# A graph layer on one core: W_tp for two groups in TensorE's column halves, placing in one pass, keys by DMA, 355 picked tiles

## The chip, the core and the metric

The kernel runs on one core of one Trainium2 chip. A core has TensorE (PE in the profile; its weight loads are PEld), VectorE (DVE), ScalarE (ACT), GpSimd (POOL) and SyncE (SP, which here only issues DMAs). The metric is the device time of one execution in microseconds; less is better. PE writes its sums to PSUM[...]; the kernel names a bank by a tag, and what is written next under a tag waits until the last reader of the tile before it is done.

## The reference

One layer of message passing over 6,250 nodes of 64 features and 200,000 edges sorted by their target, with a gate from each node's noise value, a residual and a norm over the features.

```python
w = jax.nn.silu(edge_attr @ W1 + b1) @ W2 + b2              # 200000 x 9
h_src = features[src]                                       # 200000 x 64
msg = jnp.einsum('ef,em,fmg->eg', h_src, edge_sh * w, W_tp)
agg = jax.ops.segment_sum(msg, dst, num_segments=N) / jnp.sqrt(jnp.float32(AVG_DEG))
emb = jax.nn.silu(c_noise[:, None] @ Wn1 + bn1) @ Wn2 + bn2
gamma, beta = jnp.split(emb, 2, axis=-1)
x = _layernorm(x + agg * (1.0 + gamma) + beta)
```

All values are 32-bit floats. `AVG_DEG` is 16.

## The kernel before

The 200,000 edges are 1,563 tiles of 128 edges, and 16 tiles make a group: 98 groups (`NBLK`), the last of 11 tiles. Loop `i` works on three groups at once: the hidden layer of group i + 2, the edge weights of group i + 1, the sums of group i and the projection of an older one. The order of instructions on each engine is the order in which the code is written (`manual_schedule`), so each engine's queue is laid out by hand.

**Rows of the source nodes.** A tile needs 128 rows of x. They come in three ways. POOL gathers a tile with one indirect DMA (`gather`, L91), six groups ahead (`AHEAD`) into seven buffers, so that a gather for group i + 6 needs the windows of group i - 1 to be done. Every sixth group (`SPG`) has one tile whose rows SP loads one by one (`load_rows`, L106), 22 rows in an iteration. And the last three tiles of a group (`Q`, `picked`) are picked on PE (`pick`): x lies in SBUF, split in two float32r numbers `xs`; a one-hot mask of the row within a block (`hot_k`, L464, on DVE) times `xs` gives seven candidates per feature, in 14 matmuls of 448 columns (L482); DVE then keeps one of seven (`xm`, L491) and adds up (L493) into the group's rows `hs`. The keys that the masks compare with are spread over the partitions by a matmul of ones with two bfloat16 parts of the key (`keys`, L458); the node gate (`gate`, L357) is done in the same bank.

**Per group.** `hidden` (L405, bank p1) and its Silu on ACT (L413); `second` (L422, bank s); `weights`: two transposes (L432), the product with sh (L438) and with a one-hot of 8 target positions (L444) on DVE. `windows` (L511): for each tile, rows times weights, 16 matmuls of 64 columns that write the two halves of the partitions in turn; ACT copies the sums to `zt` (L521). `project` (L537): five products of `zt` with `wtc2`, the two-at-a-time form of W_tp, each moving 64 columns; the result `r` is copied by ACT (L542). `place` (L559): two products with a one-hot `c` (L544) carry the 128 window sums of the group to two blocks of 128 nodes, and DVE adds them to `acc`, which holds all nodes (L563). `finish` gates, adds the residual and normalises two blocks of nodes (`finish_nodes`, L622 to L639): nine instructions on DVE and a square root on ACT, whose table differs from Silu's and is loaded each time (L635); the loop does this in every fourth iteration, after the second pick.

A 32-bit product runs as two passes, a float32r product and a transpose as one; the counts of the profile show it (490 projection products stand there as 980).

`pick(g, t, other)` takes the small products of other steps, one after each second matmul, so that they lie between pick matmuls. In iteration i the order on PE is: pick 0 of group i + 1 with the placing of i - 2, the keys of i + 2 and the gate between its matmuls; hidden i + 2; second i + 1; windows i; pick 1 with the weights of i + 1 and the projection of i - 1; pick 2. `setup` does the same for the first groups and splits x; `reach` tests once that the windows suffice (else a general path, not taken here, does all the work).

```python
for i in range(NBLK):
    if i + AHEAD < NBLK:
        gather(i + AHEAD)
    ...
    pick(i + 1, 0, [place(i - 2)] + ([keys(i + 2, i - 2)] if i + 2 < NBLK else []))
    ...
    hidden(i + 2)
    ...
    second(i + 1)
    ...
    windows(i)
    ...
    pick(i + 1, 1, [weights(i + 1), project(i - 1)])
    ...
    pick(i + 1, 2)
```

Of the kernel before, what the change touches and what calls it, by code (L numbers as in the profile page):

```python
# [9 lines left out]
BF16 = mybir.dt.bfloat16  # L10
# [18 lines left out]
Q = 3  # L29
# [15 lines left out]
def lo_block(g):  # L45

    return (g - 1) // 2


def picked(g):  # L50

    return Q

# [6 lines left out]
def gnn_resnorm_kernel(ctx: ExitStack, tc: tile.TileContext, x, src, dst, dst_row, ea, sh, cn,  # L60
# [18 lines left out]
    with ExitStack() as fast:  # L79
# [28 lines left out]
        acc = keep.tile([P, NJ, F], F32)  # L108
        ident = keep.tile([P, P], F32)
        w2p = keep.tile([P, D], F32)  # L110
# [7 lines left out]
        ones2 = keep.tile([P, P], BF16)  # L118
        kr2 = [keep.tile([P, LB, Q, P], BF16, name=f"kr{k}") for k in range(2)]
        zt = [keep.tile([P, 5, KB, W], F32, name=f"zt{k}") for k in range(2)]  # L120
# [7 lines left out]
        kd = dram.tile([2, C, P], BF16, name="kd")  # L128
# [7 lines left out]
        def setup(temp):  # L136
# [51 lines left out]
            nc.vector.tensor_scalar(ident, nf[:, 0:P], pf, None, op0=ALU.is_equal)  # L188
            zero = temp.tile([P, 1], F32)
            nc.vector.memset(zero, 0.0)  # L190
            for k in range(2):
                nc.vector.memset(kr2[k], 0.0)
            nc.vector.memset(ones2, 0.0)
            nc.vector.memset(ones2[0:2], 1.0)
            for k in range(2):
                nc.vector.memset(zt[k][F:P, 4], 0.0)
                nc.vector.memset(ht[k][H:H + 1], 1.0)
# [9 lines left out]
            acc_r = acc.rearrange("p j f -> p (j f)")  # L207
            s_f, kp, kh, rest, t0, t1 = [acc_r[:, k * C:(k + 1) * C] for k in range(6)]
# [12 lines left out]
            nc.vector.tensor_scalar(kh, ti[1], float(P), None, op0=ALU.mult)  # L221
            for c0 in range(0, C, P):
                n = min(P, C - c0)
                p_kt = psum.tile([P, 2, P], F32, tag=("s", "r", "s")[c0 // P], name=f"p_kt{c0}")
                for i, half in enumerate((kp, kh)):
                    nc.tensor.matmul(p_kt[0:n, i, :], half[:, c0:c0 + n], ident, start=True, stop=True)
                kt = temp.tile([P, 2, P], BF16, name=f"kt{c0}")
                nc.scalar.copy(kt[0:n], p_kt[0:n])
                nc.sync.dma_start(kd[:, c0:c0 + n, :].rearrange("i c e -> c i e"), kt[0:n])
# [36 lines left out]
            def between(h):  # L266
# [5 lines left out]
                elif h == 1:  # L272
                    for f in keys(0, -1):
                        f()
# [29 lines left out]
            for f in keys(1, -1):  # L304
                f()
# [13 lines left out]
            nc.scalar.copy(acc_r, zero.to_broadcast([P, NJ * F]))  # L319
            pick(0, 2)  # L320
# [35 lines left out]
        def gate(j, pe):  # L356
            nc.tensor.matmul(pe, ht[j // 4 % 2][:, j % 4], wn2a, start=True, stop=True)  # L357
# [5 lines left out]
        def finish(j0, j1):  # L363
            finish_nodes(nc, late, eps, acc[:, j0:j1, :], gam[:, j0:j1, :], xb[:, j0:j1, :],
                         out_v[:, j0:j1, :], j0)
# [25 lines left out]
        def load_keys(g):  # L391
            n = min(LB, NBLK - g)
            kr = kr2[g // LB % 2]
            nc.sync.dma_start(kr[0:2, 0:n].rearrange("i g t e -> i (g t) e"), kd[:, g * Q:(g + n) * Q, :])
# [56 lines left out]
        def keys(g, j):  # L451

            pk = psum.tile([P, Q + 1, P], F32, tag="r", name=f"pk{g}")
            q = picked(g)

            def part(k):
                if k == 0:
                    nc.tensor.matmul(pk[:, 0:q, :].rearrange("p t e -> p (t e)"), ones2,  # L458
                                     kr_t.pop(g).rearrange("i t e -> i (t e)"), start=True, stop=True)
                else:  # L460
                    gate(j, pk[:, Q, :])
# [62 lines left out]

        r, hot = {}, {}

        def project(g):

            if not 0 <= g < NBLK:
                return []  # L530
# [283 lines left out]
```

## Time and profile before

| | |
|---|---|
| time, median of 3 runs | 1590.99 us (1590.33 to 1592.33) |
| the profiled execution: its time, its span | 1590.71 us, 1588.9 us |
| mean granted TensorE clock | 0.961 |
| DMA | 85.42 MB, mean 54 GB/s |
| PE, 100 to 300 us: busy | 191.42 of 200 us |
| PE, 310 to 1540 us: busy | 1092.56 of 1230 us |
| POOL gathers | 1,253 |
| picked tiles | 294 |

The page gives busy time by engine, the chain of work that ended last and the costliest groups of instructions. In a group's line stand: line, engine, operation, output <- inputs, shape, count, then busy time and mean ns of one, then the idle time of the engine just before them and what ended it. A line of the timeline gives start and length in us, engine, line, operation and shape, and in brackets the idle time before it. PE's matmuls are pipelined: the length of a line is longer than the step from one start to the next, and the step is what PE pays. Idle time called "issue" is time in which the engine waited for nothing that the profile shows.

### The profile page before, as it was taken

Reading aid. Unit: us, or ns where it says so; the run is one execution under the profiler, and the core shown is the slowest. Engines: PE = TensorE matmul, PEld = TensorE weight load, DVE = VectorE, ACT = ScalarE, POOL = GpSimd, SP = SyncE. Lnnn points to the kernel's source line nnn. Section 1 sums busy time; section 2 is a strip of 40 time slices with the busy share of each in tenths; the row PEclk is TensorE's granted clock in tenths of the full one; section 3 lists DMA queues with packets and bytes.
Section 4 is the critical chain, followed back from the end, with each engine's and each line's share of the span. In section 5 each row is a group of like instructions: output and inputs, shape, how many; then the busy total and the mean of one; then the engine's idle time right before and its main releaser. Section 6 shows DMA issues by size and latency. Waiting matters only on the chain.

```text
span 1588.9 us, 33055 instructions
## 1 busy us (share of the span) xinstructions
PE 1407.5 (89%) x10206; PEld 1143.1 (72%) x10206; DVE 992.6 (62%) x1611; ACT 473.1 (30%) x1187; POOL 1186.0 (75%) x1262
## 2 busy tenths in 40 slices
PE   5999999988989888989898989888889899888886
PEld 3777778767777777777676767676777777776765
DVE  6676667665656565665665656656566666565664
ACT  4323223323232323232322323323223232322232
POOL 7777777777777777777777777777777777777773
PEclk9999999999999999999999999999999999999998
DMA  5312222221211121212111221121111211211110
GB/s 155 84 48 50 62 50 54 58 50 50 61 50 50 45 66 45 50 50 61 48 47 45 52 57 47 47 62 46 45 47 47 62 46 47 62 47 45 47 46 20
DMA packets 86199, 85.42 MB, mean 54 GB/s; under 512 B 37625, under 2 KB 52013, under 8 KB 86014
## 3 DMA queue, kind: packets, MB, share of 16 engines
q0 software_dynamic: 40096, 41.14, 11.7%
q1 hardware_dynamic: 45156, 40.44, 8.4%
q8 instruction: 83, 1.36, 0.4%
q10 hardware_dynamic: 762, 1.64, 0.3%
q14 instruction: 102, 0.84, 0.2%
HBM read 81.35 MB, written 1.78 MB: 52 GB/s over the span
## 4 chain that ended last, share of the span: by engine, by line
PE 33%; POOL 32%; issue 14%; DMA 10%; SPq 7%; DVE 2%; ACT 1%; POOLq 0%; ACTq 0%; DVEq 0%
POOL hs L91 32%; PE px L482 21%; DMA hs<-in_x_dram,src_i 9%; SPq L106 4%; PE pz L511 4%; PE pr L537 2%; PE p L405 2%; SPq L101 2%; PE p L422 1%; PE p L432 1%; PE pd L559 1%; DMA ea<-in_ea_dram 1%; DVE xm L491 0%; DVE hs L493 0%; PE pk L458 0%
## 5 line engine op out<-in xcount | busy, mean ns | idle before, releaser
L91 POOL DMA_INDIRECT hs<-in_x_dram,src_i x1253 | 1184.7, 945 | 382.6 <-issue 347.3
L482 PE MATMUL px<-xs,hot_k 128*128 128x448 f32 x4116 | 1100.4, 400 | 3.2 <-DVE xs L299 3.2
L482 PEld LDWEIGHTS px<-xs,hot_k 128*128 128x128 f32 x4116 | 717.9, 196 | 62.1 <-DVE xs L299 3.6
L491 DVE SCALAR_TENSOR_TENSOR xm<-li,jl,px 128x448 f32<-128x448 f32 x294 | 199.1, 677 | 213.0 <-PE px L482 211.2
L464 DVE TENSOR_TENSOR hot_k<-pk,nk 128x2688 fp32r<-128x2688 f32 x98 | 289.4, 2953 | 4.6 <-PE pk L458 4.6
L413 ACT ACTIVATE st<-p,b1c 128x1024 f32<-128x1024 f32 x98 | 109.1, 1114 | 560.1 <-PE p L405 559.9
L511 PE MATMUL pz<-a,hs 128*64 128x72 f32 x3126 | 135.0, 245 | 134.0 <-DMA hs<-in_x_dram,src_i 79.7
L521 ACT COPY zt<-pz 64x160 f32<-64x160 f32 (+2 forms) x784 | 213.4, 272 | 128.9 <-PE pz L511 110.8
L511 PEld LDWEIGHTS pz<-a,hs 128*64 128x64 f32 x3126 | 121.1, 151 | 177.5 <-issue 161.6
L438 DVE TENSOR_TENSOR p<-p,sh 128x72 f32<-128x72 f32 x196 | 47.3, 241 | 296.0 <-PE p L432 224.3
L537 PEld LDWEIGHTS pr<-wtc,zt 128*128 128x128 f32 x980 | 190.0, 196 | 20.8 <-ACT zt L521 5.2
L493 DVE TENSOR_REDUCE hs<-xm 128x64 f32<-128x448 f32 x294 | 182.3, 620 | 10.1
L537 PE MATMUL pr<-wtc,zt 128*128 128x64 f32 x980 | 165.0, 252 | 5.0 <-ACT zt L521 5.0
L444 DVE TENSOR_TENSOR a<-oh,p 128x1152 f32<-128x1152 f32 x98 | 132.6, 1354 | 3.3
L405 PE MATMUL p<-ea,w1bd 64*128 64x512 f32 x392 | 113.5, 657 | 5.6 <-DMA ea<-in_ea_dram 5.5
L542 ACT COPY r<-pr 128x64 f32<-128x64 f32 x98 | 20.8, 212 | 261.3 <-PE pr L537 261.3
L559 PEld LDWEIGHTS pd<-r,c 128*128 128x128 f32 x388 | 73.1, 190 | 7.3 <-ACT r L542 1.0
L422 PEld LDWEIGHTS p<-st,w2p 128*32 128x32 f32 x784 | 15.6, 109 | 74.3 <-issue 72.1
L559 PE MATMUL pd<-r,c 128*128 128x64 f32 x388 | 64.6, 249 | 0.7 <-ACT r L542 0.7
L422 PE MATMUL p<-st,w2p 128*32 128x256 f32 x784 | 63.5, 396 | 0.0
L432 PE MATMUL p<-ident,p2s 128*128 128x128 f32 x196 | 58.9, 301 | 3.9 <-ACT p2s L425 3.8
L413 ACT ACT_TABLE_LOAD x23 | 29.5, 1283 | 94.7 <-PE p L405 94.7
(103 smaller groups left out, 456.6 us busy)
## 6 DMA issues: line engine op xcount, KB each, us to landing
hs<-in_x_dram SPq DMA_DIRECT2D x2048, 0.2 KB
ea<-in_ea_dram SPq DMA_DIRECT2D x49, 512.0 KB
hs<-in_x_dram,src_i POOLq DMA_INDIRECT x1253
sh<-in_sh_dram SPq DMA_DIRECT2D x49, 144.0 KB
cb<-cn_d SPq DMA_DIRECT2D x12, 128.0 KB
out_dram<-o SPq DMA_DIRECT2D x24, 64.0 KB
gam<-in_x_dram ACTq DMA_DIRECT2D x2, 448.0 KB
dst_i<-in_dst_dram SPq DMA_DIRECT2D x1, 784.0 KB
```

The source lines that it names most:

```text
L91: hs_dma[g] = [nc.gpsimd.indirect_dma_start(out=hs[g][:, t - g * KB, :], out_offset=None, in_=x, in_offset=bass.IndirectOffsetOnAxis(ap=sr ...
L405: nc.tensor.matmul(p1[:, i, :], w1bd[i * 64:(i + 1) * 64, :], e[i * 64:(i + 1) * 64, :], start=True, stop=True)
L413: nc.scalar.activation(st[g], p1_t.pop(g), AF.Silu, bias=b1c)
L444: nc.vector.tensor_mul(a[g], oh_t.pop(g)[:, :, None, :].to_broadcast([P, KB, M, W]), sw.unsqueeze(3).to_broadcast([P, KB, M, W]))
L464: nc.vector.tensor_tensor(hot_k[g][:, 0:q], pk[:, 0:q].unsqueeze(2).to_broadcast([P, q, J, P]), nk[:, None, :, None].to_broadcast([P, q, J ...
L482: nc.tensor.matmul(px.rearrange("p f l -> p (f l)"), hot_k[g][:, t, h, :], xs[i][:, h].rearrange("p f l -> p (f l)"), start=(h == 0 and i ...
L491: nc.vector.scalar_tensor_tensor(xm, li[:, None, :].to_broadcast([P, F, J]), jl[:, c:c + 1], px, op0=ALU.is_equal, op1=ALU.mult)
L493: nc.vector.tensor_reduce(hs[g][:, tiles(g) - q + t, :], xm, AX.X, ALU.add)
L511: mm = nc.tensor.matmul(pz[v * F:(v + 1) * F, k // 2].rearrange("p m w -> p (m w)"), hsg[:, k0 + k, :], ag[:, k0 + k].rearrange("p m w -> ...
L521: nc.scalar.copy(z[h * F:(h + 1) * F, 0:5 - h, k0 + v:k0 + n:2, :].rearrange("p m k w -> p k m w"), pz[v * F:(v + 1) * F, 0:(n + 1 - v) // ...
L537: nc.tensor.matmul(pr[g], z[:, c].rearrange("p k w -> p (k w)"), wtc2[:, c, :], start=(c == 0), stop=(c == 4))
L559: nc.tensor.matmul(pd[g][:, j, :], hot[g][:, j * P:(j + 1) * P], r[g], start=True, stop=True)
```

## The change

- `Q` becomes 4, and `picked` gives 3 for three groups of eight and 4 for the other five: 355 picked tiles in all, 1,192 gathers.
- The keys are stored as one float16 number each, and SP's load spreads them over all partitions; ACT copies them to PSUM (`keys`), and the masks are made for one pick at a time (`hots`), two ahead of pick 0 of the iteration and the rest behind it.
- `project` works for two groups, in every second iteration, right behind the windows. W_tp is now the loaded operand (64 columns) and `zt` (four of them now) the moving one: group h writes half h of the partitions of bank p1, which the hidden layer uses too. ACT copies the 128 x 128 result, PE transposes it (`turn`), and `halves` splits it into two float32r numbers that lie side by side.
- `place` multiplies each group's two halves with its one-hot, 256 nodes at once, and both groups add up in PSUM. The upper 128 nodes are carried to the next pair, and the lower ones are complete (`yt`): `acc` goes.
- `bring` turns a block of nodes back and adds the two halves, with two stacked identities, and `finish` reads it from PSUM. Two blocks are finished in every fourth iteration, now within pick 0.
- `nodes` holds gate, placing and bringing of an iteration in one tile of bank s, the bank that `second` writes next.

```diff
-Q = 3
+Q = 4
...
+def pair(q):
+    return [g for g in (2 * q - 1, 2 * q) if 0 <= g < NBLK]
...
-    return Q
+    return Q - (3 * g % 8 < 3)
...
+            kf = s_f
+            nc.vector.tensor_add(kf, kp, kh)
...
+                nc.tensor.transpose(p_kt[0:n], kf[:, c0:c0 + n], ident)
...
+                nc.sync.dma_start(kd[c0:c0 + n, :], kt[0:n])
...
-                    for f in keys(0, -1):
-                        f()
+                    keys(0)
+                    hots(0, 0, Q)
...
+            keys(1)
+            hots(1, 0, Q)
...
+            for t in range(2, Q):
+                pick(0, t)
...
         def gate(j, pe):
-            nc.tensor.matmul(pe, ht[j // 4 % 2][:, j % 4], wn2a, start=True, stop=True)
             nc.vector.tensor_scalar(gam[:, j, :], pe[:, 0:F], 1.0, 0.25, op0=ALU.add, op1=ALU.mult)
             nc.vector.tensor_add(xb[:, j, :], xb[:, j, :], pe[:, F:2 * F])
...
-        def finish(j0, j1):
-            finish_nodes(nc, late, eps, acc[:, j0:j1, :], gam[:, j0:j1, :], xb[:, j0:j1, :],
-                         out_v[:, j0:j1, :], j0)
+        def finish(j0, j1, sums):
+            y = late.tile([P, j1 - j0, F], F32, tag="y", name=f"y{j0}")
+            finish_nodes(nc, late, eps, sums, y, gam[:, j0:j1, :], xb[:, j0:j1, :], out_v[:, j0:j1, :], j0)
...
         def load_keys(g):
             n = min(LB, NBLK - g)
-            kr = kr2[g // LB % 2]
-            nc.sync.dma_start(kr[0:2, 0:n].rearrange("i g t e -> i (g t) e"), kd[:, g * Q:(g + n) * Q, :])
+            kr = loads.tile([P, LB, Q, P], F16, tag="kr", name=f"kr{g}", bufs=2)
+            nc.sync.dma_start(kr[:, 0:n].rearrange("p g t e -> p (g t e)"),
+                              rows(kd[g * Q:(g + n) * Q, :].rearrange("c e -> (c e)"), P))
...
-        def keys(g, j):
-            pk = psum.tile([P, Q + 1, P], F32, tag="r", name=f"pk{g}")
-            q = picked(g)
...
-                if k == 0:
-                    nc.tensor.matmul(pk[:, 0:q, :].rearrange("p t e -> p (t e)"), ones2,
...
-                    gate(j, pk[:, Q, :])
...
+        pk_t = {}
+        def keys(g):
+            pk_t[g] = psum.tile([P, Q, P], F32, tag="r", name=f"pk{g}")
+            nc.scalar.copy(pk_t[g][:, 0:picked(g), :], kr_t.pop(g))
+        def hots(g, t0, t1):
+            for t in range(t0, min(t1, picked(g))):
+                hot_k[g, t] = late.tile([P, J, P], F32R, tag="hot_k", name=f"hot_k{g}_{t}", bufs=7)
+                nc.vector.tensor_tensor(hot_k[g, t], pk_t[g][:, t, None, :].to_broadcast([P, J, P]),
+                                        nk.unsqueeze(2).to_broadcast([P, J, P]), op=ALU.is_equal)
...
-                    nc.tensor.matmul(px.rearrange("p f l -> p (f l)"), hot_k[g][:, t, h, :],
+                    nc.tensor.matmul(px.rearrange("p f l -> p (f l)"), hot_k[g, t][:, h, :],
...
-            z = zs[g] = zt[g % 2]
+            z = zs[g] = zt[:, g % 4]
...
-        r, hot = {}, {}
-        def project(g):
-            if not 0 <= g < NBLK:
+        r, hot, carry, yt = {}, {}, {}, {}
+        def halves(q, pr):
+            n = len(pair(q))
+            r[q] = work.tile([P, 2, 2, F], F32R, tag="r", name=f"r{q}")
+            nc.scalar.copy(r[q][:, 0:n, 0], pr)
+            nc.vector.tensor_sub(r[q][:, 0:n, 1], pr, r[q][:, 0:n, 0].bitcast(F32))
+            for g in pair(q):
+                hot[g] = work.tile([P, 2 * P], F32R, tag="c", name=f"c{g}")
+                nc.vector.tensor_scalar(hot[g], nf, nid[:, g:g + 1], None, op0=ALU.is_equal)
+        def project(q):
+            gs = pair(q)
+            pt = psum.tile([P, 2, 4 * P], F32, tag="p1", name=f"pt{q}")
+            z = [zs.pop(g).rearrange("p c k w -> p c (k w)") for g in gs]
+            if len(gs) == 1:
+                for c in range(5):
+                    nc.tensor.matmul(pt[:, 0, 0:F], z[0][:, c], wtc2[:, c, :], start=(c == 0), stop=(c == 4))
+                halves(q, pt[:, 0, 0:F].unsqueeze(1))
                 return []
-            pr = {}
...
-                    pr[g] = psum.tile([P, F], F32, tag="r", name=f"pr{g}")
-                nc.tensor.matmul(pr[g], z[:, c].rearrange("p k w -> p (k w)"), wtc2[:, c, :],
-                                 start=(c == 0), stop=(c == 4))
...
-        def place(g):
...
+            for c in range(5):
+                for h in range(2):
+                    nc.tensor.matmul(pt[h * F:(h + 1) * F, 0, 0:P], wtc2[:, c, :], z[h][:, c],
+                                     start=(c == 0), stop=(c == 4))
+            rt = work.tile([P, P], F32, tag="rt", name=f"rt{q}")
+            nc.scalar.copy(rt, pt[:, 0, 0:P])
+            def turn():
+                nc.tensor.transpose(pt[:, 1, 0:P], rt, ident)
+                halves(q, pt[:, 1, 0:P].rearrange("p (g f) -> p g f", g=2))
+            return [lambda: None, lambda: None, turn]
+        def place(q, pd):
+            gs = pair(q)
+            def part(k):
+                nc.tensor.matmul(pd, r[q][:, k].rearrange("p s f -> p (s f)"), hot.pop(gs[k]),
+                                 start=(k == 0), stop=(k == len(gs) - 1))
+                if k == len(gs) - 1:
+                    r.pop(q)
+                    if q > 0:
+                        yt[q - 1] = work.tile([P, P], F32, tag="yt", name=f"yt{q}", bufs=3)
+                        nc.vector.tensor_add(yt[q - 1], pd[:, 0:P], carry.pop(q - 1))
+                    if q < NJ:
+                        carry[q] = work.tile([P, P], F32, tag="carry", name=f"carry{q}")
+                        nc.scalar.copy(carry[q], pd[:, P:2 * P])
+            return [lambda k=k: part(k) for k in range(len(gs))]
...
+        def bring(j0, j1, py):
             def part(j):
-                if j == js[0]:
-                    pd[g] = psum.tile([P, 2, F], F32, tag="s", name=f"pd{g}")
-                nc.tensor.matmul(pd[g][:, j, :], hot[g][:, j * P:(j + 1) * P], r[g], start=True, stop=True)
-                if j == js[-1]:
-                    hot.pop(g), r.pop(g)
-                    b0, b1_ = kb + js[0], kb + js[-1] + 1
-                    nc.vector.tensor_add(acc[:, b0:b1_, :], acc[:, b0:b1_, :], pd[g][:, js[0]:js[-1] + 1, :])
...
-        done = 0
+                nc.tensor.matmul(py[:, j - j0], yt.pop(j), ident2, start=True, stop=True)
+                if j == j1 - 1:
+                    finish(j0, j1, py[:, 0:j1 - j0])
+            return [lambda j=j: part(j) for j in range(j0, j1)]
+        def nodes(i):
+            ps = psum.tile([P, 4, P], F32, tag="s", name=f"ps{i}")
+            parts = []
+            if 0 <= i - 2 < NJ:
+                def product(j=i - 2):
+                    nc.tensor.matmul(ps[:, 2], ht[j // 4 % 2][:, j % 4], wn2a, start=True, stop=True)
+                parts.append(product)
+            if i % 2 == 0 and i >= 2:
+                parts += place(i // 2 - 1, ps[:, 0:2].rearrange("p a n -> p (a n)"))
+            j = (i - 5) // 2
+            if i % 2 == 1 and i >= 5 and j % FB == FB - 1:
+                parts += bring(j + 1 - FB, j + 1, ps[:, 3].rearrange("p (j f) -> p j f", f=F))
+            if 0 <= i - 2 < NJ:
+                parts.append(lambda: gate(i - 2, ps[:, 2]))
+            return parts
...
@@ -582,7 +614,12 @@
                 for g in SPG:
                     if 0 < g - i <= AHEAD:
                         load_rows(g, (AHEAD - g + i) * SPR)
-                pick(i + 1, 0, [place(i - 2)] + ([keys(i + 2, i - 2)] if i + 2 < NBLK else []))
+                if i + 2 < NBLK:
+                    keys(i + 2)
+                    hots(i + 2, 0, 2)
+                pick(i + 1, 0, [nodes(i)])
+                if i + 2 < NBLK:
+                    hots(i + 2, 2, Q)
                 if 3 <= i <= 5:
                     reach(i - 3)
                 if i + 2 < NBLK:
@@ -591,25 +628,32 @@
                     second(i + 1)
                 if i < NBLK - 2:
                     windows(i)
+                turn = project(i // 2) if i % 2 == 1 else []
                 if i % 4 == 1 and i - 1 < NJ:
                     gate_hidden(i - 1)
                 if i + 1 < NBLK:
-                    pick(i + 1, 1, [weights(i + 1), project(i - 1)])
-                else:
-                    for f in project(i - 1) + place(i - 1):
+                    pick(i + 1, 1, [weights(i + 1), turn])
+                for t in range(2, Q):
+                    pick(i + 1, t)
+                if i == NBLK - 1:
+                    for f in turn:
                         f()
-                ready = max(lo_block(i if i == NBLK - 1 else i - 1), 0)
-                while ready - done >= (FB if ready < NJ - 1 else 1):
-                    finish(done, min(done + FB, ready))
-                    done = min(done + FB, ready)
-                pick(i + 1, 2)
+                    ps = psum.tile([P, 4, P], F32, tag="s", name="ps_l")
+                    for f in place(i // 2, ps[:, 0:2].rearrange("p a n -> p (a n)")):
+                        f()
+                    py = psum.tile([P, FB, F], F32, tag="r", name="py_l")
+                    for f in bring(NJ - 3, NJ - 1, py):
+                        f()
                 if i >= NBLK - 2:
                     windows(i)
                 if i == NBLK - 2:
                     sums(i + 1)
-            for f in project(NBLK - 1) + place(NBLK - 1):
+            project(NBLK // 2)
+            ps = psum.tile([P, 4, P], F32, tag="s", name="ps_n")
+            for f in place(NBLK // 2, ps[:, 0:2].rearrange("p a n -> p (a n)")):
                 f()
-            finish(done, NJ)
+            for f in bring(NJ - 1, NJ, psum.tile([P, 1, F], F32, tag="r", name="py_n")):
+                f()
...
-def finish_nodes(nc, work, eps, y, gam, xb, out, tag):
+def finish_nodes(nc, work, eps, sums, y, gam, xb, out, tag):
     n = y.shape[1]
-    nc.vector.tensor_mul(y, y, gam)
+    nc.vector.tensor_mul(y, sums, gam)
     nc.vector.tensor_add(y, y, xb)
...
```

## The prediction

> **What bounds the kernel now.** I read the busy shares first, then the costliest groups, the chain that ended last, the timeline of a dense stretch and that of the end.
>
> ```profile
> PE 1407.5 (89%) x10206; PEld 1143.1 (72%) x10206; DVE 992.6 (62%) x1611; ACT 473.1 (30%) x1187; POOL 1186.0 (75%) x1262
> ...
> PE 33%; POOL 32%; issue 14%; DMA 10%; SPq 7%; DVE 2%; ACT 1%; POOLq 0%; ACTq 0%; DVEq 0%
> ...
> L91 POOL DMA_INDIRECT hs<-in_x_dram,src_i x1253 | 1184.7, 945 | 382.6 <-issue 347.3
> L482 PE MATMUL px<-xs,hot_k 128*128 128x448 f32 x4116 | 1100.4, 400 | 3.2 <-DVE xs L299 3.2
> L464 DVE TENSOR_TENSOR hot_k<-pk,nk 128x2688 fp32r<-128x2688 f32 x98 | 289.4, 2953 | 4.6 <-PE pk L458 4.6
> L511 PE MATMUL pz<-a,hs 128*64 128x72 f32 x3126 | 135.0, 245 | 134.0 <-DMA hs<-in_x_dram,src_i 79.7
> ```
>
> POOL looks 75% busy and is full: busy plus the idle before its gathers is 1184.7 + 382.6 = 1567.3 us of 1588.9, and that idle is "issue", not a wait. One gather costs 1567.3/1253 = 1.2508 us. PE looks fuller, but waits in the windows (L511) for gathered rows. So POOL sets the pace: 12.8 gathers, 16.0 us a group.
>
> How much PE has to spare is read where it is not waiting, in the first 300 us, where it works off a late start:
>
> ```profile
> 224.96 1.22 PE L511 MATMUL pz<-a,hs 128*64 128x72 f32 x32
> 227.65 0.33 PE L537 MATMUL pr<-wtc,zt 128*128 128x64 f32 x2
> 228.28 0.33 PE L537 MATMUL pr<-wtc,zt 128*128 128x64 f32 x2
> 230.32 3.54 PE L482 MATMUL px<-xs,hot_k 128*128 128x448 f32 x16
> 233.70 0.33 PE L559 MATMUL pd<-r,c 128*128 128x64 f32 x2
> 237.08 1.13 PE L405 MATMUL p<-ea,w1bd 64*128 64x512 f32 x4
> 238.14 0.64 PE L422 MATMUL p<-st,w2p 128*32 128x256 f32 x8
> 238.71 1.22 PE L511 MATMUL pz<-a,hs 128*64 128x72 f32 x32
> ```
>
> From windows to windows 13.75 us, and starts give prices: a pick's matmul (233.70 - 230.32)/16 = 0.211 us, so a pick of 14 is 2.96; a projection product, 0.63 less two pick matmuls, 0.21; the hidden layer 1.06; the second 0.57; the windows 1.15. The same reading gives 0.21 for a placing product, 0.15 for the keys, 0.27 for the node gate and 0.09 for a transpose.
>
> ```profile
> 1545.91 1.22 PE L511 MATMUL pz<-a,hs 128*64 128x72 f32 x32
> 1566.57 1.22 PE L511 MATMUL pz<-a,hs 128*64 128x72 f32 x32
> 1571.34 0.66 PE L559 MATMUL pd<-r,c 128*128 128x64 f32 x4 [0.35 <-ACT r L542]
> 1576.71 2.40 PE L537 MATMUL pr<-wtc,zt 128*128 128x64 f32 x10 [3.68 <-ACT zt L521]
> ```
>
> After the windows of group 95, at 1545.9, PE runs dense once more; from there to the end are 43.0 us.
>
> **What the Trainium skill says.** "TensorE: Matmul & The Clock Gate", Part 3, lets matmuls with different column tiles run at once, and its section on LDWEIGHTS prices a load by columns, P/1.2 ns. The trace agrees with the second: a projection pass, loading 128 columns and moving 64, takes 0.21/2 = 0.105 us, where the page gives 107 ns. For the first it agrees in part: the windows, 64-column halves in turn, take 1.15/32 = 36 ns a pass, far below 105, not half of the page's 53 ns for a load. "TensorEngine Tiling (Array Packing)", Key Properties, says that changing the tiling mode drains the array; the new block stands right behind the windows, which use the same halves. "ScalarE: Activation LUTs", "What ACT_TABLE_LOAD costs", gives 1283 ns for the load alone; the trace's mean is 1283. "TensorE", Part 1, lets the clock fall after an idle window of about 3.4 us; here it was 0.66 after a wait from 836 to 839 us and 1.00 after one of 2.6 us at 823.
>
> **The change, part by part.**
>
> *Picks.* 294 become 355, groups of 3 and 4. POOL loses 61 gathers, 61 x 1.2508 = 76.3 us. PE gains 61 x 2.96 = 180 us. DVE gains 61 x (xm 0.68 + reduce 0.62 + hot 1.0, a third of L464's 2.95) = 140 us, to some 1130 of 1500: it keeps up, but its order matters below.
>
> *Projection.* 97 x 5 products of 0.21 (102 us) become 48 blocks of ten products in column halves, two passes each, 128 columns moved. At the windows' 36 ns a block is 20 x 36 = 0.72 us; stretched by 128/72, 1.28. I take 0.9; bounds 0.7 and 1.5. A turn is one transpose, 0.09. Its copies on ACT and DVE lie beside the picks that follow: the transpose comes only after five pick steps, 2.1 us. Without that cover some 0.6 us a pair, 30 in all.
>
> *Placing and nodes.* 194 placing products of 0.21 become 98 single passes moving 256 columns. The nearest row, the pick's matmul, moves 448 in 0.211; by columns 256 give 0.12, and as a part of it won't shrink I take 0.13, bounds 0.1 and 0.2. Bringing back adds 49 products of 0.21. The gate stays.
>
> *Keys.* PE loses 98 x 0.15; ACT gains 98 copies of 512, about the 0.47 us of the 256-wide p2s row or a little more, ahead of need and beside PE's picks (49 us if they were on the path). SP's one load of keys a pair stays one, now 256 KB, against 656 KB of ea and sh; the DMA engines are 20% busy. In setup the copy stands in ACT's queue ahead of the xs copies and waits for the key load: I put the first windows at 53.5 us instead of 50.96.
>
> *SP.* Each group has 22 row loads; the store of finished nodes now waits earlier in its iteration (in every fourth), so the ea load behind it comes sooner. The waits of L405 for ea (11 us on PEld) should go; no gain is booked.
>
> *New waits.* Hot masks of two picks (2.0 us), then the finishing of nodes, now stand on DVE ahead of the gate. In every fourth iteration: DVE takes the last pick's xm and reduce until 1.46 us after PE's first pick starts (in the dense stretch that pick starts at 233.28, DVE is free at 234.74), hots to 3.46, finish 2.97 (1572.36 to 1575.33 in the tail of before) to 6.4, gate 0.35 to 6.8. The bank of these sums is the one that `second` needs; PE arrives there after 2.96 + 0.27 + 0.42 + 1.06 = 4.7 us and waits 2.1. Behind `second` stand the windows and every later pick. Where no gate is left (from iteration 51) the bank is free sooner, but the projection now shares the bank of the hidden layer: the square root at 5.6, 0.29, the table load 1.28 and the activation 1.11 end at 8.3, while PE comes at 6.15 and waits 2.2. Either way about 2.1 us, 23 times: 48 us. Below nothing isn't possible for a wait; nothing is, where PE already waits for rows.
>
> **The sum.** PE from the first windows to those of group 95: 345 picks x 2.958 = 1020.5; 95 x (1.06 + 0.57 + 1.15 + 0.18) = 281; 49 gates 13.2; 47 blocks and turns x 0.99 = 46.4; 93 placings 12.1; 46 bringings 9.5: 1382. With 48 of waits, 6 for the range check (before lost 5.9 there: 19.6 us from 104.03 to 123.64 instead of 13.75), from 53.5: 1489.5. The rest takes 43.0 + 3.0 (a pick more) - 1.8 (projection and placing) + 3.8 (a pair, its turn, halves, bringing, before the last windows and again after) = 48. Span 1537.5; the profiled execution lies 1.8 above its span, and at 1590.71 is 0.3 under the median of 1590.99. **1539 us.**
>
> POOL alone: group 95's rows come 60 gathers sooner, 75 us; 1470.9 + 48 + 1.8 = 1521. PE starts three groups behind and POOL may run six ahead, so neither waits for the other until the slower has run its course: the larger sum holds.
>
> **The rivals.**
> *POOL still sets it* (0.22): 1521. For it: PE's lead over it is 18 us in 1400, and if half of the 2.1 us waits is absent or the block costs 0.5 us, it is gone. Against: each link of those waits is priced from a row.
> *The clock falls* (0.12): each 2.1 us wait tips the clock as at 836 us, where windows took 2.19 instead of 1.22; some 1.6 us each, 23 times: 1575. Against: the 2.6 us wait at 823 us left it at 1.00.
> *Slower* (0.08): the halves don't overlap and each pass costs what a projection pass costs now, 0.105; a block is 2.1 us, 48 x 1.2 = 58 more, 1597. It decides from 2.05 us a block. Against: the windows' 36 ns.
> That the change doesn't do what it says is no rival: its products and gathers are counted in the program.
>
> **How the numbers follow.** Likeliest (0.58): 1539, its own range 1526 to 1556 from the block's 0.7 to 1.5 us and placing's 0.1 to 0.2. For 8 in 10, low takes in POOL's case, 1516; high goes toward the clock's, 1568. Faster by over 0.2% (what a measurement here can tell): 0.90; within 0.2%: 0.02; slower: 0.08.
>
> **What would show it.** POOL's gathers 1192 at 1.25 us, but now with idle time that waits for PE or ends early; PE waiting for DVE or ACT 2 us once in four groups at `second` or at the first product of the block, hardly for rows; a block of about 0.9 us; first windows at 53.5. It is wrong if PE still waits for gathered rows in the last third (then 1521), or if PE's clock is below 0.95 in the mean.

## The result and the profile after

The changed kernel takes 1567.8 us (median of 4 runs, 1563.3 to 1570.09); the kernel before, beside it, 1591.62 (4 runs, 1590.33 to 1592.33). The ratio is 0.9848 (0.9823 to 0.9872): 23.8 us less, where 52 were forecast. The profiled execution took 1570.09 us, its span is 1568.3 at a mean clock of 0.972. The page of the kernel after:

```profile
PE 1460.5 (93%) x10810; PEld 1208.6 (77%) x10810; DVE 1139.5 (73%) x1987; ACT 528.6 (34%) x1335; POOL 1129.5 (72%) x1201
...
PE 51%; POOL 20%; DVE 13%; issue 8%; DMA 4%; ACT 3%; SPq 0%; DVEq 0%; POOLq 0%; ACTq 0%
...
L91 POOL DMA_INDIRECT hs<-in_x_dram,src_i x1192 | 1128.2, 946 | 364.0 <-issue 335.0
L475 PE MATMUL px<-xs,hot_k 128*128 128x448 f32 x4970 | 1100.8, 375 | 8.4 <-DVE xs L294 7.8
...
L460 DVE TENSOR_TENSOR hot_k<-pk,nk 128x896 fp32r<-128x896 f32 x355 | 370.5, 1081 | 2.3 <-ACT pk L454 2.3
...
L504 PE MATMUL pz<-a,hs 128*64 128x72 f32 x3126 | 125.5, 236 | 1.1 <-DMA hs<-in_x_dram,src_i 0.6
...
L543 PE MATMUL pt<-zt,wtc 128*64 128x128 f32 x960 | 72.8, 305 | 27.7 <-ACT st L411 26.0
L420 PE MATMUL p<-st,w2p 128*32 128x256 f32 x784 | 63.7, 395 | 35.7 <-DVE xb L356 32.0
```

The bound has moved as forecast. POOL's gathers, 61 fewer, cost (1128.2 + 364.0)/1192 = 1.25 us each as before, and PE's windows wait 1.1 us for rows in all, where they waited 134. PE waits elsewhere now: at `second` for DVE's `xb`, 32 us, and at the projection block for ACT's activation of the hidden layer, 26 us. The view of all waits shows a third one, ACT's for the carry, which has the largest row of that view without being PE's:

```profile
ACT carry L568 <- DVE yt L565: 384.3, 48, 9.7
...
PE p L420 <- DVE xb L356: 32.0, 34, 2.2
...
PE pt L543 <- ACT st L411: 26.0, 12, 2.2
```

(Columns: us in total, times, longest.) How these lie in time is seen in the timeline of the kernel after, here an iteration with a placing:

```profile
303.85 0.28 PE L559 MATMUL ps<-c,r 128*128 128x256 f32 x1
...
304.08 2.08 DVE L460 TENSOR_TENSOR hot_k<-pk,nk 128x896 fp32r<-128x896 f32 x2
...
306.08 0.28 DVE L565 TENSOR_TENSOR yt<-ps,carry 128x128 f32<-128x128 f32 x1
306.39 0.27 ACT L568 COPY carry<-ps 128x128 f32<-128x128 f32 x1 [6.75 <-DVE yt L565]
306.69 0.22 DVE L355 TENSOR_SCALAR gam<-ps 128x64 f32<-128x64 f32 x1 [0.33 <-ACT carry L568]
306.83 0.21 DVE L356 TENSOR_TENSOR xb<-xb,ps 128x64 f32<-128x64 f32 x1
...
307.19 0.64 PE L420 MATMUL p<-st,w2p 128*32 128x256 f32 x8 [0.38 <-DVE xb L356]
```

ACT has been idle for 6.75 us when it copies the carry, and PE's last placing product started at 303.85: the copy waits for DVE's addition, which reads the same tile and stands behind two masks on DVE. The gate then waits for the copy, and `second` for the gate. In a late stretch of the same timeline, the block twice, once without and once with a wait:

```profile
1247.56 1.26 PE L543 MATMUL pt<-zt,wtc 128*64 128x128 f32 x20
1248.75 0.67 PE L475 MATMUL px<-xs,hot_k 128*128 128x448 f32 x2
...
1262.01 8.26 PE L475 MATMUL px<-xs,hot_k 128*128 128x448 f32 x40
1270.11 0.33 PE L576 MATMUL ps<-ident,yt 128*128 128x64 f32 x2
...
1275.29 0.30 ACT L679 ACTIVATE var<-var,eps 128x2 f32<-128x2 f32 x1 [10.65 <-DVE var L678]
1275.61 1.28 ACT L411 ACT_TABLE_LOAD   x1
1276.90 1.11 ACT L411 ACTIVATE st<-p,b1c 128x1024 f32<-128x1024 f32 x1
1278.07 2.20 PE L543 MATMUL pt<-zt,wtc 128*64 128x128 f32 x20 [2.16 <-ACT st L411]
1280.20 1.12 PE L475 MATMUL px<-xs,hot_k 128*128 128x448 f32 x2
```

By starts the block costs 1248.75 - 1247.56 = 1.19 us, and a pick's matmul (1270.11 - 1262.01)/40 = 0.2025 us. After the wait of 2.16 us the same block takes 2.13 us and the two pick matmuls behind it are slow too. The view by stretches says why (columns: stretch, its us, busy time of PE, PEld, DVE, ACT and POOL with counts, PE's granted clock, DMA share, GB/s):

```profile
1246.00:1270.00 24.00, 23.85 (x199) 20.35 (x198) 17.18 (x29) 10.07 (x26) 18.19 (x20) 1.00 0.18 42
1280.20:1281.50 1.30, 1.30 (x6) 1.11 (x5) 0.00 (x0) 0.57 (x3) 0.95 (x1) 0.50 0.18 47
1281.50:1290.00 8.50, 8.50 (x45) 7.68 (x43) 6.76 (x13) 0.76 (x2) 6.61 (x7) 0.99 0.13 27
```

PE stays busy and its clock is at a half for some 3.4 us in all. There are 18 such stretches in the execution, 90.6 us together, 14 of them in the loop.

The trace's record of the granted clock shows what brings such a fall on. All 18 stretches start a whole multiple of 3.413 us apart, so the falls keep a beat: time is as if cut into stretches of 3.413 us, and a fall comes only at the end of one. PE has 23 waits of 2.1 to 2.2 us, 11 at `second` and 12 at the block. In 14 of them 1.84 us or more of the wait lay within one beat, and the clock fell at that beat's end. The other nine were cut in two by a beat's end, with at most 1.64 us on one side, and no fall followed. (Of the other four stretches, two lie in the setup, one behind the range check's wait of 4.81 us and one at the end.)

### The profile page after: what moved, and what is told of

It reads as the page before. It is cut to its first block, busy times and chain, and to the rows that moved or that the text cites. A ratio compares the mean times of both kernels' runs of the same rounds, so it can differ in the third digit from the quotient of the medians.

```text
span 1568.3 us, 34363 instructions
## 1 busy us (share of the span) xinstructions
PE 1460.5 (93%) x10810; PEld 1208.6 (77%) x10810; DVE 1139.5 (73%) x1987; ACT 528.6 (34%) x1335; POOL 1129.5 (72%) x1201
## 3 DMA queue, kind: packets, MB, share of 16 engines
q10 hardware_dynamic: 762, 1.64, 0.3%
## 4 chain that ended last, share of the span: by engine, by line
PE 51%; POOL 20%; DVE 13%; issue 8%; DMA 4%; ACT 3%; SPq 0%; DVEq 0%; POOLq 0%; ACTq 0%
PE px L475 37%; POOL hs L91 20%; DVE hot_k L460 5%; PE pz L504 5%; DMA hs<-in_x_dram,src_i 4%; PE pt L543 3%; PE p L420 2%; DVE xm L484 2%; DVE hs L486 2%; PE p L403 1%; PE p L430 1%; ACT L411 1%; ACT st L411 1%; DVE oh L382 1%; ACT carry L568 1%
## 5 line engine op out<-in xcount | busy, mean ns | idle before, releaser
L91 POOL DMA_INDIRECT hs<-in_x_dram,src_i x1192 | 1128.2, 946 | 364.0 <-issue 335.0
L475 PEld LDWEIGHTS px<-xs,hot_k 128*128 128x128 f32 x4970 | 903.3, 190 | 96.7 <-issue 12.2
L484 DVE SCALAR_TENSOR_TENSOR xm<-li,jl,px 128x448 f32<-128x448 f32 x355 | 240.4, 677 | 220.2 <-PE px L475 217.9
L460 DVE TENSOR_TENSOR hot_k<-pk,nk 128x896 fp32r<-128x896 f32 x355 | 370.5, 1081 | 2.3 <-ACT pk L454 2.3
L486 DVE TENSOR_REDUCE hs<-xm 128x64 f32<-128x448 f32 x355 | 220.1, 620 | 12.5 <-DVE xm L484 0.2
L568 ACT COPY carry<-ps 128x128 f32<-128x128 f32 x48 | 12.7, 265 | 390.2 <-DVE yt L565 382.4
L543 PE MATMUL pt<-zt,wtc 128*64 128x128 f32 x960 | 72.8, 305 | 27.7 <-ACT st L411 26.0
L543 PEld LDWEIGHTS pt<-zt,wtc 128*64 128x64 f32 x960 | 62.2, 157 | 29.7 <-ACT st L411 27.8
L454 ACT CAST pk<-kr 128x384 f32<-128x384 f16 (+1 forms) x98 | 53.9, 550 | 1.5 <-DMA kr<-kd 1.4
L403 PEld LDWEIGHTS p<-ea,w1bd 64*128 64x128 f32 x392 | 30.2, 188 | 28.8 <-issue 27.9
```

What stands on the lines that cost most here:

```text
L91: hs_dma[g] = [nc.gpsimd.indirect_dma_start(out=hs[g][:, t - g * KB, :], out_offset=None, in_=x, in_offset=bass.IndirectOffsetOnAxis(ap=sr ...
L403: nc.tensor.matmul(p1[:, i, :], w1bd[i * 64:(i + 1) * 64, :], e[i * 64:(i + 1) * 64, :], start=True, stop=True)
L460: nc.vector.tensor_tensor(hot_k[g, t], pk_t[g][:, t, None, :].to_broadcast([P, J, P]), nk.unsqueeze(2).to_broadcast([P, J, P]), op=ALU.is_ ...
L475: nc.tensor.matmul(px.rearrange("p f l -> p (f l)"), hot_k[g, t][:, h, :], xs[i][:, h].rearrange("p f l -> p (f l)"), start=(h == 0 and i ...
L484: nc.vector.scalar_tensor_tensor(xm, li[:, None, :].to_broadcast([P, F, J]), jl[:, c:c + 1], px, op0=ALU.is_equal, op1=ALU.mult)
L486: nc.vector.tensor_reduce(hs[g][:, tiles(g) - q + t, :], xm, AX.X, ALU.add)
```

## The experiments

The theory, A: PE is the bound, and what is missing of the gain are waits of PE that the order on DVE and ACT makes, and the clock that falls after the longer ones. The rivals: the new products on PE themselves cost what is missing, or the pick does; the last is answered from the traces alone.

**Masks behind the pick (e1).** Two of the 1 us masks leave the way of the gate, the placing's readers and the finish on DVE; the others move from behind pick 0 to behind pick 1.

```diff
-                    hots(i + 2, 0, 2)
                 pick(i + 1, 0, [nodes(i)])
                 if i + 2 < NBLK:
-                    hots(i + 2, 2, Q)
+                    hots(i + 2, 0, 2)
...
                     pick(i + 1, 1, [weights(i + 1), turn])
+                if i + 2 < NBLK:
+                    hots(i + 2, 2, Q)
```

> The masks of two picks, which stood on DVE ahead of the placing sums, the finishing and the gate, are made behind pick 0 instead, those of the other picks behind pick 1; nothing else. Theory A (PE sets the end: its products plus the waits at `second` and at the projection block for banks s and p1, which DVE's masks make late, plus the clock that falls after these waits): the waits of 2.0 us (iterations 7 to 47, every fourth), 2.3 us (the same later) and 0.2 to 0.45 us (even iterations), 69 us together, and most of the clock's falls go, PE's sum falls under POOL's, and POOL sets the end: 1518 to 1530 us, with PE waiting for gathered rows. Theory B (PE is bound by its products alone, the waits are spare time): 1560 to 1570. Theory C (POOL sets the end already): no change, 1568.

1520.38 us (1519.98 to 1520.85), ratio 0.9549 (0.9533 to 0.9565): 47 us below the changed kernel with the same instructions. A row of the page of e1, and its timeline in an iteration that finishes nodes:

```profile
L504 PE MATMUL pz<-a,hs 128*64 128x72 f32 x3126 | 124.0, 234 | 26.6 <-issue 11.2
...
1284.92 0.30 ACT L680 ACTIVATE var<-var,eps 128x2 f32<-128x2 f32 x1 [1.32 <-DVE var L679]
...
1285.23 1.28 ACT L411 ACT_TABLE_LOAD   x1
...
1285.30 0.64 PE L420 MATMUL p<-st,w2p 128*32 128x256 f32 x8
...
1286.35 0.94 POOL L91 DMA_INDIRECT hs<-in_x_dram,src_i  x1 [0.30 <-issue]
...
1286.53 1.11 ACT L411 ACTIVATE st<-p,b1c 128x1024 f32<-128x1024 f32 x1
...
1291.11 2.19 PE L504 MATMUL pz<-a,hs 128*64 128x72 f32 x32 [5.17 <-issue]
```

The activation ends at 1287.6, and PE reaches its block later. What PE waits for now are rows again, 26.6 us in all. The trace names no releaser for the 5.17 us ahead of the windows at 1291, but the last gather of that group began at 1286.35. The windows of group 95 start at 1471.59, where the prediction had put POOL's route alone at 1470.9. So the order of the masks held back all that lay between PE's bound and POOL's.

**The gate ahead (e2).** The gate's two DVE instructions are put right behind its product, ahead of the placing and bringing.

```diff
                 parts.append(product)
+                parts.append(lambda: gate(i - 2, ps[:, 2]))
...
-            if 0 <= i - 2 < NJ:
-                parts.append(lambda: gate(i - 2, ps[:, 2]))
```

> The gate's two instructions on DVE go ahead of bringing and finishing; the masks stay in front. Theory A, where a wait that is taken away at `second` meets the next one: up to iteration 50 the wait at `second` falls from 2.0 us to nothing, and at the projection block, where bank p1 is held by the hidden layer's activation behind square root and table load, about 2.2 us come instead, as they already do after iteration 50: 1562 to 1570. Rival (the waits are separate costs): 12 x 2.0 us and the clock's falls behind them go, 1530 to 1545.

1663.43 us (1653.03 to 1665.61), ratio 1.0426 (1.0388 to 1.0463): 96 us above the changed kernel; neither theory had it. The timeline of e2:

```profile
329.36 2.08 DVE L460 TENSOR_TENSOR hot_k<-pk,nk 128x896 fp32r<-128x896 f32 x2
331.36 0.22 DVE L355 TENSOR_SCALAR gam<-ps 128x64 f32<-128x64 f32 x1
331.49 0.21 DVE L356 TENSOR_TENSOR xb<-xb,ps 128x64 f32<-128x64 f32 x1
331.85 0.36 PE L559 MATMUL ps<-c,r 128*128 128x256 f32 x1 [2.66 <-DVE xb L356]
```

The wait at `second` did shrink, from 2.2 us to 0.1, but placing writes the tile that the gate reads, so PE now stops inside pick 0 until DVE has made its masks and the gate. PE's wait for `xb` in front of placing alone is 66.5 us, in front of bringing 24.6, and the clock is at a half in 33 stretches, 145 us. A reader moved ahead of a writer of the same tile makes the writer wait.

**zt as the loaded operand (e3).** As before the change: 128 columns loaded, 64 moved, and so no turn.

```diff
-            for c in range(5):
-                for h in range(2):
-                    nc.tensor.matmul(pt[h * F:(h + 1) * F, 0, 0:P], wtc2[:, c, :], z[h][:, c],
+            for h in range(2):
+                for c in range(5):
+                    nc.tensor.matmul(pt[:, 1, h * F:(h + 1) * F], z[h][:, c], wtc2[:, c, :],
```

> The projection of a pair as before the change (the window sums loaded, 128 columns, W_tp moved, 64 columns), still as one block of ten products and split as now; column halves and turn go. Theory A: a block takes 2.1 us instead of 1.2, the turn's 0.13 goes, and as PE sets the end all of it shows: 48 x 0.78 = 37 us more, 1598 to 1608. Theory C (POOL sets the end): under 5 us.

1639.05 us (1632.27 to 1641.33), ratio 1.028 (1.0254 to 1.0306): 71 above the changed kernel, where 30 to 40 were expected. The timeline of e3, the block without a wait ahead of it:

```profile
1304.67 2.44 PE L543 MATMUL pt<-wtc,zt 128*128 128x64 f32 x20
1306.93 0.66 PE L475 MATMUL px<-xs,hot_k 128*128 128x448 f32 x2
```

2.26 us, 113 ns a pass, against 1.19. Less a transpose of 0.11 that goes, 48 x (1.07 - 0.11) = 46 us. The rest, 25, goes with the clock: 142 us at a half instead of 91. The 23 long waits are those of the changed kernel, but in the loop 12 of 17 falls last 6.8 us or more, where all but one lasted 3.4; why is not shown. The block by itself costs about what the rival *Slower* had set, 1.07 us more against its 1.2.

**Three picks a group (e4).** `picked` returns 3 throughout: 294 picked tiles and 1,253 gathers, as before, in the new structure.

```diff
-    return Q - (3 * g % 8 < 3)
+    return Q - 1
```

> All groups pick 3 tiles, 294 in all and 1253 gathers as before the change; the rest of the change stays. Theory A: PE loses 61 picks of 2.84 us, 173 us, and is far from the bound; POOL sets the end as before the change: 1588 to 1596, PE waiting for rows. Rival (the new projection, placing and keys are worth time by themselves): under 1580.

1594.56 us (1591.68 to 1596.55), ratio 1.0018 (1.0011 to 1.0025). The page of e4:

```profile
L91 POOL DMA_INDIRECT hs<-in_x_dram,src_i x1253 | 1185.8, 946 | 382.8 <-issue 350.4
...
L504 PE MATMUL pz<-a,hs 128*64 128x72 f32 x3126 | 151.4, 263 | 167.5 <-DMA hs<-in_x_dram,src_i 120.3
```

With as many gathers as before, the time is that of before but for 3 us: without fewer gathers, the rest of the change gains nothing, and the windows wait 167.5 us for rows instead of 134.0. That the rest is what pays for the picks is a reckoning, not a run: 61 picks at the 2.8 us that are measured below are some 171 us of PE (an estimate), more than those 134. The kernel before with 355 picks was not run.

**The first four on another chip (e5 to e8).** Four kernels were first run on a chip where the kernel before itself took 2373.06 us instead of 1591, with POOL waiting for PE and DVE idle for causes that the traces of e5 to e8 name only "remote". There the changed order of the carry took 2525.68, the halves in turn 2541.81, the filler 2535.6 and 361 picks with the masks behind 2464.73. What slows that chip was not found. All four were run again beside a kernel before of 1591.13 us (9 runs, 1589.89 to 1592.7), and only these are read below. They are compared with the changed kernel's 1567.8 us, whose own kernel before took 1591.62, 0.5 us more.

**The carry first (e9).** ACT's copy is written ahead of DVE's addition; nothing else changes.

```diff
-                    if q > 0:
-                        yt[q - 1] = work.tile([P, P], F32, tag="yt", name=f"yt{q}", bufs=3)
-                        nc.vector.tensor_add(yt[q - 1], pd[:, 0:P], carry.pop(q - 1))
                     if q < NJ:
                         carry[q] = work.tile([P, P], F32, tag="carry", name=f"carry{q}")
                         nc.scalar.copy(carry[q], pd[:, P:2 * P])
+                    if q > 0:
+                        yt[q - 1] = work.tile([P, P], F32, tag="yt", name=f"yt{q}", bufs=3)
+                        nc.vector.tensor_add(yt[q - 1], pd[:, 0:P], carry.pop(q - 1))
```

> The kernel of e5 again, as the chip of e5 to e8 ran the kernel before at 2373 us. In placing, ACT's copy of the upper 128 nodes is written ahead of DVE's addition of the lower ones; the changed kernel otherwise. Theory A (the 0.2 to 0.45 us at `second` in even iterations come from three readers of one bank that are put in a row: addition on DVE, copy on ACT, gate on DVE): ACT copies at once, the row is one link shorter, `second` waits about 0.25 us less in each of 47 even iterations: 8 to 14 us less than the 1567.8 of the changed kernel, and ACT's idle time ahead of the copy, 382 us, goes. Rival (the wait is for the masks alone): under 3 us.

1541.47 us (1539.96 to 1545.82), ratio 0.9687 (0.9674 to 0.9701): 26 below the changed kernel, twice what was expected. The timeline of e9:

```profile
1267.63 0.27 ACT L565 COPY carry<-ps 128x128 f32<-128x128 f32 x1 [4.01 <-PE ps L559]
...
1270.16 0.28 DVE L568 TENSOR_TENSOR yt<-ps,carry 128x128 f32<-128x128 f32 x1
1270.61 0.64 PE L420 MATMUL p<-st,w2p 128*32 128x256 f32 x8
```

The copy follows PE's placing at once, and in the even iterations `second` hardly waits any more. From start to start, the last of the hidden layer to the first of `second` falls from 0.95 to 0.54 us in the first half of the even iterations and from 0.74 to 0.52 in the second: 25 x 0.41 + 22 x 0.22 = 15 us. Most of the other 11 goes with the clock: 13 slow stretches of 73 us instead of 18 of 91, half of which is 9. That part isn't shown to be the exchange's own work: all 23 long waits are still there, as long as they were, and 9 instead of 14 of them bring a fall, as they lie elsewhere on the beat.

**The halves one after the other (e10).** The two loops of the block change places: five products in the lower half of the columns, then five in the upper.

```diff
-            for c in range(5):
-                for h in range(2):
+            for h in range(2):
+                for c in range(5):
```

> The kernel of e6 again. The ten products of a pair's projection are ordered by group, five in the lower half of the columns and then five in the upper, instead of in turn. If the two halves run beside each other when they alternate, a block of 1.2 us grows to 1.6 to 2.1 us, 20 to 45 us in all: 1588 to 1613. If they don't, and 60 ns a pass is simply the time of 128 columns moved: 1.2 us as now, 1564 to 1572.

1600.18 us (1597.68 to 1603.0), ratio 1.0062 (1.0047 to 1.0078): 32 above the changed kernel. The timeline of e10:

```profile
1267.41 1.97 PE L543 MATMUL pt<-zt,wtc 128*64 128x128 f32 x20
1269.31 0.67 PE L475 MATMUL px<-xs,hot_k 128*128 128x448 f32 x2
```

1.90 us instead of 1.19; 48 x 0.71 = 34, near the 32 measured. A pass costs 95 ns one after the other and 60 ns alternated. The Trainium skill, "TensorE: Matmul & The Clock Gate", Part 3, says that matmuls in different tiles of the array overlap; this pair of runs agrees, though not to a factor of two. Whether two products overlap, or a product and the next load, these runs don't tell.

**PE kept busy (e11).** In each fourth iteration, 16 products whose sum nobody reads are put ahead of `second`, where PE used to wait. Nothing is left out; work is added.

```diff
+                    if i % 4 == 3 and i >= 7:
+                        fill = psum.tile([P, 2 * P], F32, tag="pz", name=f"fill{i}", bufs=2)
+                        for k in range(16):
+                            nc.tensor.matmul(fill, xs[0][:, 0]...[:, 0:P], xs[1][:, k % J]...[:, 0:2 * P],
+                                             start=True, stop=True)
                     second(i + 1)
```

> The kernel of e7 again. In every fourth iteration from 7 on, 16 products of 256 columns that nobody reads (into a bank of the windows) stand ahead of `second`, about 2 us, where PE waits 2.0 us up to iteration 50 and 2.3 us later. It does more work in the same order. If the clock falls because PE is idle there (14 falls of 3.4 us in the loop, each some 1.7 us of work lost), the falls in the loop go and the time is 10 to 24 us less, 1544 to 1558. If the falls have another cause, the time stays or grows by up to 8 us.

1546.54 us (1544.91 to 1547.36), ratio 0.9719 (0.9706 to 0.9732): 21 us less, with 368 more products. The timeline of e11:

```profile
1255.38 2.17 PE L631 MATMUL fill<-xs,xs 128*128 128x256 f32 x16
1257.48 0.64 PE L420 MATMUL p<-st,w2p 128*32 128x256 f32 x8
...
1259.33 1.31 PE L543 MATMUL pt<-zt,wtc 128*64 128x128 f32 x20
1260.57 0.67 PE L475 MATMUL px<-xs,hot_k 128*128 128x448 f32 x2
```

The filler lasts as long as the wait did, so no wait is saved; the block behind it takes 1.24 us again. The slow stretches fall from 18 to 4 and the clock rises from 0.972 to 0.989. So some 21 us of the changed kernel are the clock's, and what lowers it is PE standing idle, not the work. The one stretch left in the loop follows the range check, which has no filler.

**The best (e12).** The masks as in e1 and six more picks, since POOL was the bound again in e1.

```diff
-    return Q - (3 * g % 8 < 3)
+    return Q - (5 * g % 16 < 5)
```

> The kernel of e8 again: the masks behind pick 0 and pick 1, and 361 picks instead of 355. POOL loses 6 gathers, 7.5 us, PE gains 17 us, of which some 27 us of waiting for rows in the second half can take most: 1511 to 1519 us against 1520.4 with 355 picks. If PE's remaining waits make it the bound at once: 1522 to 1532.

1513.38 us (1512.74 to 1515.7), ratio 0.9514 (0.9501 to 0.9527). The page of e12:

```profile
PE 82%; DVE 6%; POOL 3%; ACT 3%; issue 2%; DMA 2%; SPq 1%; DVEq 0%; ACTq 0%; POOLq 0%
...
L504 PE MATMUL pz<-a,hs 128*64 128x72 f32 x3126 | 121.1, 231 | 7.5 <-DMA hs<-in_x_dram,src_i 6.0
```

PE carries 82% of the chain and hardly waits for rows: 78 us below the kernel before, 54 below the changed one.

## Why the prediction was right in its bound and wrong in its size

Direction and bound were right: PE sets the pace, POOL's gathers cost the 1.25 us that were priced and end with room to spare. The time came out 28.8 us late, at the upper end of the range. That it was no later is luck: one error of 42 us, in the other direction, hid most of the rest. Most of the 28.8 arose in the loop, group by group as the sum had it (95 steps, from the first windows to those of group 95):

| term | forecast, us | measured, us |
|---|---|---|
| 345 picks | 1020.5 | 345 x 14 x 0.2025 = 978 |
| hidden, second, windows, transposes | 281 | 95 x 3.09 = 294 |
| gates | 13.2 | 49 x 0.24 = 12 |
| blocks and turns | 46.4 | 47 x (1.19 + 0.11) = 61 |
| placings | 12.1 | 93 x 0.115 = 11 |
| bringings | 9.5 | 11 |
| waits of about 2.1 | 48 | 11 x 2.17 + 11 x 2.36 = 50 |
| waits of the even iterations | 0 | 16 |
| range check, with the fall behind it | 6 | 7.6 |
| the clock's falls behind long waits | 0 | 13 x 1.6 = 21 |
| sum | 1436 | 1462; the trace has 1461.35 |

(The measured terms are read by starts, from iterations that differ in one thing; each is good to a few us. The forecast's parts add up to 1436.7.)

- **"about 2.1 us, 23 times: 48 us" held**, and so did its two places: `second` until the gates end, the block after. This was the longest argument of the forecast, and the trace has just these 23 waits, 11 at `second` and 12 at the block; the last of them lies behind the windows of group 95, so the table has 22.
- **The step that failed first is *New waits*: "In every fourth iteration".** Waits in the even iterations were costed at nothing. The placing's readers stand behind the same two masks, ACT's copy behind DVE's addition, the gate behind the copy, and `second` behind the gate: 16 us, of which e9 takes away 15 with one exchange of two statements.
- **The second is the rival *The clock falls*, set aside with "the 2.6 us wait at 823 us left it at 1.00".** These are that wait and the one at 836 us, in the timeline of the kernel before, whose falls keep a beat of 3.413 us too:

```profile
823.04 1.22 PE L511 MATMUL pz<-a,hs 128*64 128x72 f32 x32 [2.61 <-DMA hs<-in_x_dram,src_i]
...
839.38 2.19 PE L511 MATMUL pz<-a,hs 128*64 128x72 f32 x32 [2.75 <-issue]
```

A beat's end cut the first into 1.83 and 0.79 us, and the clock stayed up; of the second, 2.68 us lay in one beat, and the clock fell at 839.32. So the wait that was taken as evidence stayed without a fall by luck of where it lay. In the loop of the changed kernel 13 of the 22 long waits brought a fall, at 1.6 us each, just what had been read off at 836 us. Such a cost is part of the likeliest case, here with 13/22 of its full size, and no separate case. The sign that had been set for it, a mean clock below 0.95, could not tell: it is 0.972, above the 0.961 of the kernel before. e11 shows that the 21 us are the clock's: as much less, with more work.

- **Mis-sized: "I take 0.9" for the block.** 1.19 us, inside the bounds 0.7 to 1.5, 14 us in all. The windows' 36 ns stretched by the columns moved (1.28) was the nearer of the two ends.
- **Mis-sized the other way: "a pick's matmul (233.70 - 230.32)/16 = 0.211 us".** It is 0.2025 in a long run, and iterations that differ in one pick say the same: from windows to windows 14.88 us with four picks and 12.09 with three, 2.8 us for 14 matmuls. The 16 that were counted begin with one behind a projection product. In the kernel before the step of such a matmul is 0.29 us and that of the small product's last pass 0.08: part of the small product was charged to the pick. (By the same reading a projection pass of before is 0.11 us rather than 0.105.) For an iteration of before with both it made no difference, but the change adds 61 picks and drops small products, and 42 us too much were charged. This error hid most of the others.
- The likeliest case's own range was too narrow for its own bounds: a block of 1.5 us and a placing of 0.2 add 48 x 0.6 + 98 x 0.07 = 36 us, so it reaches 1575 and not 1556.
- *Keys*, *Placing* and *SP* were right in size: first windows at 55.84 instead of 53.5 (the clock is at a half for 6.8 us twice in the setup, where it was 3.4 us twice before), placing 0.115 us instead of 0.13, and no wait for ea is left. The tail took 51.1 us instead of 48: the same clock, 0.77 there, and the block's wait once more, as the timeline of the kernel after shows:

```profile
1517.19 1.22 PE L504 MATMUL pz<-a,hs 128*64 128x72 f32 x32
...
1520.56 2.34 PE L543 MATMUL pt<-zt,wtc 128*64 128x128 f32 x20 [2.15 <-ACT st L411]
```

- *POOL still sets it* was wrong for the kernel as changed and right for e1, 1520.38 us against 1521. *Slower* was wrong, as alternating halves cost 60 ns a pass; one after the other (e10) they cost 95, near the 105 that it had.

## What to carry to other kernels

When a buffer gets more users, walk every iteration through all of them, in the order in which each engine meets them, and not only the one with the longest work: two engines that read one tile are put in line by the order in which the code names them, so the idle one goes first. Where the tensor engine will be the bound, price the waits that it is given with the clock that they cost (here 13 of 22 waits of about 2.1 us, 1.6 us each: an estimate of 1 us a wait), and take the price of a product from a long run of its kind, without the first one behind a product of another kind. An order of the code on a side engine can be worth more than the change itself: here 24 us for the change and 54 for two lines of order and six more picks.

## What the runs showed of the hardware

- The Trainium skill, "TensorE: Matmul & The Clock Gate", Part 1, puts the fall of the clock behind an idle window of about 3.4 us. In the changed kernel most stretches at a half last about that long, and the falls keep a beat of 3.413 us, but a wait of 2.1 to 2.2 us is enough: 14 of 23 brought a fall, those with 1.84 us or more within one beat, and none of those with 1.64 us or less did. In other runs (e3, e9) waits with 1.6 to 1.9 us in one beat went either way. Filling the waits takes the stretches from 18 to 4 (e11).
- Ten products in two 64-column halves that alternate take 60 ns a pass of 128 moved columns, one after the other 95; with 128 columns loaded and 64 moved they take 113. So of the 53 ns between the last form and the first, 35 come with the alternation.
- Time at a half does not simply follow PE's work. With the same 23 long waits, the changed kernel has 91 us at a half, e10 with a block 0.71 us longer 77, and e3 with one 1.07 us longer 142.
